# Layer-1 context attention of a four-layer perceiver: every product but the scores split into two column halves

## The chip, the cores and the metric

The kernel runs on one core of one Trainium2 chip. A core has a matrix engine (TensorE, which the profile splits into PE, the products, and PEld, the loads of the stationary operand), a vector engine (DVE), a scalar engine (ACT), a general engine (POOL) and a queue engine that issues transfers (SP). TensorE multiplies with an array of 128 rows and 128 columns and writes into PSUM, a memory of eight banks. The rows stand for the summed index and the columns for the output's partitions. A product that needs only a part of the array can be placed in that part; the profile writes "128*64" for a product that uses 128 rows and 64 columns.

The metric is device time in microseconds, the median of several runs.

## The reference, cut to what matters

The program is a perceiver with four layers. Each layer lets 2 x 256 queries of width 256 attend over a context, then over themselves, then runs a feed-forward block. Here only layer 1's attention over the context matters. It has 16 heads of width 64 and 4096 context rows per batch:

```python
def _L1_xattn_setup():
    B, S, D = (4, 512, 256)
    H, DK, DV = (16, 64, 64)
...
x = x + _L1_xattn_ref(_layernorm(x, axis=-1), ctx_1024, ctx_1024,
                      L1_xattn_Wq, L1_xattn_bq, L1_xattn_Wk, L1_xattn_bk,
                      L1_xattn_Wv, L1_xattn_bv, L1_xattn_Wo, L1_xattn_bo)
```

For each head: q = xn Wq + bq, k = ctx Wk + bk, v = ctx Wv + bv, softmax(q k^T) v, and the heads' outputs are multiplied by Wo and added up. Everything is in fp32.

## The kernel before, in words

The method `l1_xattn` (from L973 on) works on pairs of heads: a pair fills 128 partitions, one head in the lower 64 and one in the upper 64. There are n = 16 pairs (8 per batch; `u` counts them), and each pair's 4096 context rows are taken in 8 pieces of 512, so there are G = 128 pieces, counted by `g`. The nested functions are the stages of a piece:

- `keys(g)`: kT (128 x 512) from the transposed context, two products of 512 columns, then ACT adds the bias (L1024).
- `scores(g)` (L1051): both heads side by side in the row halves of the array, since a head has only 64 rows to sum over; four PSUM banks. ACT copies the scores out (L1058), DVE keeps a running maximum (L1061).
- `less(g)`: DVE adds the negative maximum (L1072), ACT takes the exponential (L1075), POOL adds up the sums (L1086; in the last pair DVE and L1082 share this).
- `values(g)`: v (4 x 128 rows by 128) from the context, eight products of 128 columns.
- `weigh(g)` (L1098): both heads side by side in the column halves of the array, since a head has only 64 output columns.
- Once per pair: `query` makes the queries; `combine`, `turned` (L1119, four transposes), `maxima` (L1125) and `repeat` (L1130, four transposes) turn the maximum of each query into a row that `less` can add; the sums of exponentials come from a product with ones; `end` divides (L1135, L1136, L1139), and `out` multiplies by Wo.

Products go through the helper `mm` (L358), so keys, values, query, out and sums all bear that line; the transposes of `turned` and `repeat` are calls of the transpose operation. Every fp32 product is two records in the profile, with a load each; a transpose is one.

The loop at L1158 writes the order out by hand, and `in_order` (L1157) fixes it for PE, DVE, ACT and POOL. In step g it issues `weigh(g-10)`, then `out` (when g % 8 is 2) or `query` (5), half of `less(g-9)`, `end` (1), `keys(g+1)`, `turned` (0), the other half of `less(g-9)`, `maxima` (0), `values(g-9)`, `repeat` (0) and `scores(g)`. The stage has PSUM banks 4 "mm" (scores, query, turned, sums, out), 2 "tr" (keys, values), 1 "acc" (weigh) and 1 "dec" (repeat). Context pieces are loaded by SP three steps ahead (L1006). In the first steps there is nothing to weigh; after step 128 there are only values, weigh and less.

Of the kernel before, what the change touches and what calls it, by code (L numbers as in the profile page):

```python
# [22 lines left out]
P = 128  # L23
B = 2
L = 256
# [4 lines left out]
KC = D // P  # L30
# [238 lines left out]
class Perceiver:  # L269
# [85 lines left out]
    def mm(self, out, pairs):  # L355

        for i, (lhsT, rhs) in enumerate(pairs):
            self.nc.tensor.matmul(out, lhsT, rhs, start=i == 0, stop=i == len(pairs) - 1)  # L358
# [614 lines left out]
    def l1_xattn(self, x, cpool):  # L973
# [9 lines left out]
        nc = self.nc  # L983
        with ExitStack() as s:
# [3 lines left out]
            xnT = self.to_T(self.layernorm(x))  # L988
            wq, wk, wv, wo = (self.weight(f"l1x_w{n}") for n in "qkvo")
# [8 lines left out]
            halves = [slice(0, 64), slice(64, 128)]  # L998
            order = [(hh, i) for i in range(2) for hh in range(2)]
            ctx, q, kT, v, score = {}, {}, {}, {}, {}  # L1000
            most, low, spread, total, av, sums, rec, z = {}, {}, {}, {}, {}, {}, {}, {}
# [7 lines left out]
            def for_values(g):  # L1009

                return ("k", g + 8) if g + 8 < G and (g + 8) // 64 == g // 64 else ("v", g)

            def query(u):
                ps = self.bank([P, L])
                self.mm(ps, [(wq[:, k, ts(u % 8, P)], xnT[:, k, ts(u // 8, L)]) for k in range(KC)])
                q[u] = p2.tile([P, L], F32, name="qT", tag="qT")
                return lambda: nc.vector.tensor_scalar_add(q[u], ps, self.col("l1x_bq", u % 8))

            def keys(g):
                pr = g // 8 % 8  # L1020
                ps = self.bank([P, 512], "tr")
                self.mm(ps, [(wk[:, k, ts(pr, P)], ctx["k", g][:, k, :]) for k in range(KC)])
                kT[g] = p2.tile([P, 512], F32, name="kT", tag="kT")
                nc.scalar.activation(kT[g], ps, AF.Identity, bias=self.col("l1x_bk", pr))  # L1024

            def values(g):
                pr = g // 8 % 8
                ps = self.bank([P, 4, P], "tr")
                for i in range(4):
                    self.mm(  # L1030
                        ps[:, i, :],
                        [(ctx[for_values(g)][:, k, ts(i, P)], wv[:, k, ts(pr, P)]) for k in range(KC)],
                    )
                v[g] = p2.tile([P, 4, P], F32, name="v", tag="v", bufs=3)
                self.copy(g < G - 8, v[g], ps)
# [80 lines left out]
            def turned(u):  # L1116
                ps = self.bank([P, 4, P])
                for i in range(4):
                    nc.tensor.transpose(ps[:, i, :], low[u][:, i // 2, ts(i % 2, P)], self.ident)  # L1119
                low[u] = ps  # L1120

            def maxima(u):
# [18 lines left out]
            def out(u):  # L1141
                ps = self.bank([P, 2, D])
                for qt in range(2):
                    self.mm(ps[:, qt, :], [(z[u][:, ts(qt, P)], wo[:, u % 8, :])])
                two = y[:, ts(u // 8, 2), :]
                return lambda: nc.vector.tensor_add(two, ps, two)

# [9 lines left out]
            with self.in_order(e.PE, e.DVE, e.Activation, e.Pool):  # L1157
                for g in range(-1, G + 12):  # L1158
# [7 lines left out]
                    u = g // 8 - 1 if g % 8 == 0 and 0 < g <= G else None  # L1166
# [6 lines left out]
                    if g % 8 == 2 and made(g - 11):  # L1173
                        evacs.append(out((g - 11) // 8))
                    if (g == -1 or g % 8 == 5) and made(g + 3):
                        evacs.append(query((g + 3) // 8))
# [5 lines left out]
                    if made(g + 1):  # L1182
                        keys(g + 1)
                    if u is not None:
                        turned(u)
# [6 lines left out]
                    if made(g - 9) and g <= G:  # L1192
                        values(g - 9)
                    if made(g - 8) and g >= G:
                        values(g - 8)
# [1394 lines left out]
```

## Time and profile before

| what | value |
|---|---|
| median of 3 runs | 2627.32 us (2615.05, 2627.32, 2627.75) |
| profiled execution's own time | 2616.86 us |
| its span, first to last instruction | 2615.1 us |
| mean granted TensorE clock | 0.96 (1.00 from 360 to 1236 us) |
| busy share of the span: PE, DVE, ACT, POOL | 95%, 66%, 51%, 35% |
| layer 1's context attention | about 263 to 1299 us of the span |
| its keys (PE, L358) | 512 records of 128x512, 250.6 us busy |
| its values (PE, L358) | 2048 records of 128x128, 249.9 us busy |
| its scores (PE, L1051) | 2048 records of 64x256, 255.7 us busy |
| its weigh (PE, L1098) | 2048 records of 128x256, 250.1 us busy |

Times in a profile are those of one execution. A group line names source line, engine, operation, output and inputs, shape and count. A timeline line begins with the start (us from the span's start) and the length of a run of equal instructions; the end of its last product is modelled, so the next group may start before it. In square brackets stands the idle time of the engine just before, and what ended it.

### The profile page before, as it was taken

To read this page: it belongs to the slowest core of one execution; us is meant where nothing else is said; L and a number is where in the kernel's file an instruction comes from. 1 tells how busy PE (TensorE), PEld (TensorE's weight loads), DVE (VectorE), ACT (ScalarE), POOL (GpSimd) and SP (SyncE) were. 2 spreads that over 40 slices of the span, in tenths; PEclk is the share of its full clock that TensorE was granted. 3 is DMA by queue.
4 is the path that set the end of the run, shared out by engine and by line. 5 is a ranking of instruction groups with operands and counts; after the bars stand their busy time and mean duration, and the time that the engine had idled before them with its cause. 6 is when DMAs were issued, how large, how long until landed. Compare 5 with 4: busy or idle time off the path is not lost.

```text
span 2615.1 us, 45590 instructions
## 1 busy us (share of the span) xinstructions
PE 2480.0 (95%) x17701; PEld 1659.1 (63%) x17701; DVE 1713.5 (66%) x3184; ACT 1343.4 (51%) x2540; POOL 919.3 (35%) x864
## 2 busy tenths in 40 slices
PE   8987999999999999999799998899989999999889
PEld 6854566666666666666533565556935666664678
DVE  5566577777777777777769755544267888854642
ACT  3323666666666666666466421432215777784512
POOL 0520255555555555556639413001101222210010
PEclk9988999999999999999899998789999999999889
DMA  6210322222232222222210100005730000003656
GB/s 256 89 57 30 118 65 65 67 72 65 65 113 82 70 69 65 65 67 81 80 65 1 65 20 22 4 25 214 266 147 18 2 2 2 2 2 123 218 213 223
DMA packets 77255, 214.24 MB, mean 82 GB/s; under 512 B 6408, under 2 KB 21456, under 8 KB 66544
## 3 DMA queue, kind: packets, MB, share of 16 engines
q1 hardware_dynamic: 72128, 202.69, 23.4%
q0 software_dynamic: 1888, 5.90, 0.7%
q8 instruction: 139, 2.28, 0.4%
q10 hardware_dynamic: 3024, 2.75, 0.3%
q14 instruction: 76, 0.62, 0.1%
HBM read 190.48 MB, written 20.84 MB: 81 GB/s over the span
## 4 chain that ended last, share of the span: by engine, by line
PE 39%; DVE 6%; issue 2%; ACT 2%; POOL 2%; DMA 0%; another core or an unknown queue 0%; DVEq 0%; ACTq 0%; POOLq 0%; SPq 0%
PE ps_mm L358 10%; PE ps_mm L2172 5%; PE ps_tr L2216 5%; PE ps_tr L2200 4%; PE ps_tr L358 3%; PE acc L358 3%; PE ps_mm L785 2%; DVE state L1357 1%; POOL spread L1345 1%; PE ps_tr L2335 1%; PE acc L826 1%; PE ps_tr L801 1%; PE ps_tr L2378 1%; PE ps_mm L2360 1%; PE acc L1583 1%
## 5 line engine op out<-in xcount | busy, mean ns | idle before, releaser
L1086 POOL TENSOR_TENSOR total<-total,S 128x512 f32<-128x512 f32 x434 | 540.8, 1278 | 299.6 <-ACT S L1075 299.2
L1075 ACT ACTIVATE S<-S 128x512 f32<-128x512 f32 x512 | 302.3, 625 | 209.0 <-DVE S L1072 208.8
L2176 DVE TENSOR_REDUCE mx<-ps_mm 128x1 f32<-128x512 f32 x512 | 317.9, 684 | 73.0 <-PE ps_tr L2200 54.2
L1061 DVE TENSOR_TENSOR most<-ps_mm,most 128x512 f32<-128x512 f32 x448 | 278.3, 684 | 119.2 <-ACT S L1058 119.2
L1058 ACT COPY S<-ps_mm 128x512 f32<-128x512 f32 x512 | 262.8, 600 | 115.3 <-PE ps_mm L1051 114.5
L1072 DVE TENSOR_TENSOR S<-S,ps_dec 128x512 f32<-128x512 f32 x512 | 317.6, 680 | 1.3 <-PE ps_dec L1130 1.3
L2204 ACT ACTIVATE PT<-ps_tr 128x512 f32<-128x512 f32 x476 | 246.7, 603 | 74.6 <-PE ps_tr L2200 71.8
L358 PEld LDWEIGHTS ps_tr<-w_l1x_wv,ctxT 128*128 128x128 f32 x2048 | 246.9, 192 | 52.5 <-issue 52.2
L1051 PE MATMUL ps_mm<-qT,kT 64*128 64x256 f32 x2048 | 255.7, 389 | 0.0
L1098 PE MATMUL acc<-S,v 128*64 128x256 f32 x2048 | 250.1, 385 | 0.5 <-DVE rec L1136 0.4
L358 PE MATMUL ps_tr<-ctxT,w_l1x_wk 128*128 128x512 f32 x512 | 250.6, 612 | 0.0
L2172 PE MATMUL ps_mm<-kT,qT 32*128 32x512 f32 x1024 | 250.1, 618 | 0.2 <-DVE mx L2176 0.2
L358 PE MATMUL ps_tr<-w_l1x_wv,ctxT 128*128 128x128 f32 x2048 | 249.9, 275 | 0.0
L2200 PE MATMUL ps_tr<-qm,kT 32*128 32x256 f32 x1904 | 238.3, 388 | 0.0
L1051 PEld LDWEIGHTS ps_mm<-qT,kT 64*128 64x128 f32 x2048 | 187.3, 186 | 38.3 <-DVE most L1061 3.8
L1098 PEld LDWEIGHTS acc<-S,v 128*64 128x64 f32 x2048 | 136.1, 136 | 97.3 <-ACT S L1058 38.8
L2200 PEld LDWEIGHTS ps_tr<-qm,kT 32*128 32x128 f32 x1904 | 171.0, 184 | 15.6 <-issue 6.2
L2225 POOL TENSOR_TENSOR sums<-sums,part 128x256 f32<-128x256 f32 x102 | 73.7, 722 | 257.1 <-ACT part L2224 257.1
L358 PEld LDWEIGHTS ps_tr<-ctxT,w_l1x_wk 128*128 128x128 f32 x512 | 89.2, 189 | 100.6 <-issue 99.1
L335 DVE COPY v<-ps_tr 128x512 f32<-128x512 f32 x120 | 82.9, 690 | 89.0 <-PE ps_tr L358 88.9
L2216 PE MATMUL ps_tr<-PT,v 128*32 128x256 f32 x2048 | 139.6, 385 | 0.3 <-ACT PT L2204 0.3
L2172 PEld LDWEIGHTS ps_mm<-kT,qT 32*128 32x128 f32 x1024 | 86.3, 185 | 61.3 <-issue 49.9
(542 smaller groups left out, 3808.8 us busy)
## 6 DMA issues: line engine op xcount, KB each, us to landing
ctxT<-in_ctxT SPq DMA_DIRECT2D x144, 512.0 KB, 3.6
ctxT<-in_ctxT SPq DMA_DIRECT2D x16, 1024.0 KB, 5.7
w_l2f_gu<-in_l2f_gu SPq DMA_DIRECT2D x16, 1024.0 KB, 7.1
bd_dram<-bd SPq DMA_DIRECT2D x8, 1536.0 KB, 5.5
w_l3f_w<-in_l3f_w SPq DMA_DIRECT2D x11, 1028.0 KB, 9.8
w_l3f_w<-in_l3f_w SPq DMA_DIRECT2D x11, 1024.0 KB, 5.1
ctx<-in_ctx SPq DMA_DIRECT2D x8, 1024.0 KB, 4.9
w_l2f_down<-in_l2f_down SPq DMA_DIRECT2D x16, 512.0 KB, 5.3
```

The source lines that it names most:

```text
L358: self.nc.tensor.matmul(out, lhsT, rhs, start=i == 0, stop=i == len(pairs) - 1)
L1051: nc.tensor.matmul(banks[hh, i][:, j, :], k[part, ts(2 * i + j, P)], q[u][part, :], start=True, stop=True)
L1058: nc.scalar.copy(t, ps)
L1061: nc.vector.tensor_tensor(m, ps, m, ALU.max)
L1072: nc.vector.tensor_tensor(t, t, spread[u][:, hh, :].unsqueeze(1).to_broadcast([P, 2, L]), ALU.add)
L1075: nc.scalar.activation(t, t, AF.Exp)
L1086: nc.gpsimd.tensor_add(tot, tot, t)
L1098: nc.tensor.matmul(av[u][part], vs[:, 2 * i + j, part], got[hh, i][:, j, :], start=g % 8 == 0 and i + j == 0, stop=g % 8 == 7 and i + j == 2,)
L2172: nc.tensor.matmul(ps, qT[rows, 2 * half + c, ts(t, P)], kT[rows, ts(j, 512)], start=True, stop=True,)
L2176: nc.vector.tensor_reduce(mx[:, c, r, j : j + 1], ps, AX.X, ALU.max)
L2200: nc.tensor.matmul(ps[:, i, :], kT[rows, ts(2 * u + i, P)], q[rows], start=True, stop=True)
L2216: nc.tensor.matmul(ps[ts(r, 32), :], v[:, 2 * u + i, :], pt[:, i, :], start=i == 0, stop=i == 1)
```

## The change

A local `mm` takes the place of the helper in `query`, `keys`, `values`, `turned` and `out`. It splits the stationary operand's 128 columns into two halves of 64 and the output's partitions likewise, and issues the two halves of each pair of operands one after the other; both halves stream the same second operand. `turned` no longer uses the transpose operation: it multiplies the maxima (stationary) by the identity. `scores`, `weigh`, the sums and `repeat` are as they were.

```diff
+            def mm(ps, pairs):
+
+                for k, (a, b) in enumerate(pairs):
+                    for part in halves:
+                        nc.tensor.matmul(ps[part], a[:, part], b, start=k == 0, stop=k == len(pairs) - 1)
+
             def query(u):
                 ps = self.bank([P, L])
-                self.mm(ps, [(wq[:, k, ts(u % 8, P)], xnT[:, k, ts(u // 8, L)]) for k in range(KC)])
+                mm(ps, [(wq[:, k, ts(u % 8, P)], xnT[:, k, ts(u // 8, L)]) for k in range(KC)])
...
             def keys(g):
                 pr = g // 8 % 8
                 ps = self.bank([P, 512], "tr")
-                self.mm(ps, [(wk[:, k, ts(pr, P)], ctx["k", g][:, k, :]) for k in range(KC)])
+                mm(ps, [(wk[:, k, ts(pr, P)], ctx["k", g][:, k, :]) for k in range(KC)])
...
                 for i in range(4):
-                    self.mm(
+                    mm(
                         ps[:, i, :],
                         [(ctx[for_values(g)][:, k, ts(i, P)], wv[:, k, ts(pr, P)]) for k in range(KC)],
                     )
...
             def turned(u):
                 ps = self.bank([P, 4, P])
                 for i in range(4):
-                    nc.tensor.transpose(ps[:, i, :], low[u][:, i // 2, ts(i % 2, P)], self.ident)
+                    mm(ps[:, i, :], [(low[u][:, i // 2, ts(i % 2, P)], self.ident)])
                 low[u] = ps
...
             def out(u):
                 ps = self.bank([P, 2, D])
                 for qt in range(2):
-                    self.mm(ps[:, qt, :], [(z[u][:, ts(qt, P)], wo[:, u % 8, :])])
+                    mm(ps[:, qt, :], [(z[u][:, ts(qt, P)], wo[:, u % 8, :])])
```

## The prediction

> **What bounds the kernel now.** I first looked up the stage that the change touches, the layer-1 context attention, which runs from 263 us (first L358 key product) to 1299 us of the span. The busy times by window give its steady part:
>
> ```profile
> 360.00:1236.00 876.00, 874.83 (x6043) 606.00 (x6042) 654.14 (x1047) 547.58 (x1003) 511.81 (x412) 1.00 0.25 72
> ```
>
> Columns: window, length, then PE, PEld, DVE, ACT, POOL busy (instructions), granted clock, DMA share, GB/s. TensorE is busy 874.8 of 876.0 us, VectorE, the next, 654 (75%). So time here is TensorE's time, and the question is what lies between its instructions, since a busy PE is not PE at its peak. The timeline of one ordinary step g, TensorE alone:
>
> ```profile
> 787.09 1.95 PE L1098 MATMUL acc<-S,v 128*64 128x256 f32 x16
> 788.96 1.98 PE L358 MATMUL ps_tr<-ctxT,w_l1x_wk 128*128 128x512 f32 x4
> 790.78 1.95 PE L358 MATMUL ps_tr<-w_l1x_wv,ctxT 128*128 128x128 f32 x16
> 792.66 2.00 PE L1051 MATMUL ps_mm<-qT,kT 64*128 64x256 f32 x16
> ```
>
> The next weigh starts at 794.59: a step lasts 7.50 us: weigh 1.87, keys 1.82, values 1.88, scores 1.93. The array's shape (rows*columns in use) is 128*64, 128*128, 128*128, 64*128: three changes of shape per step. Their price shows in two other places of the same view, where one of these groups has a neighbour of its own shape:
>
> ```profile
> 1254.63 1.95 PE L1098 MATMUL acc<-S,v 128*64 128x256 f32 x16
> 1256.41 1.08 PE L358 MATMUL ps_mm<-total,ones 128*64 128x256 f32 x8
> ...
> 822.03 1.88 PE L358 MATMUL ps_tr<-ctxT,w_l1x_wk 128*128 128x512 f32 x4
> 823.75 1.95 PE L358 MATMUL ps_tr<-w_l1x_wv,ctxT 128*128 128x128 f32 x16
> ```
>
> Weigh followed by the sums (128*64 too) takes 1.78, not 1.87; keys after the 128*128 product of `out` take 1.72, not 1.82. So the change of shape from weigh to keys costs 0.09 before the first key product and 0.10 after it, 0.20 us in the single records (0.310 instead of 0.213 to the first start, 0.533 instead of 0.429 to the second). The instructions by tile confirm the second half (min/median/max ns):
>
> ```profile
> L358 PEld LDWEIGHTS ps_tr<-w_l1x_wv,ctxT x2048: 186/192/192, 305.1 to 1284.5; 128*128 128x128 f32 x187
> L358 PE MATMUL ps_tr<-w_l1x_wv,ctxT x2048: 272/275/377, 305.5 to 1284.6; 128*128 128x128 f32 x187
> L358 PE MATMUL ps_tr<-ctxT,w_l1x_wk x512: 592/592/697, 262.7 to 1236.4; 128*128 128x512 f32 x171
> ```
>
> The longest key product, the one behind a change, is 105 ns over the median.
>
> **What the Trainium skill says.** "TensorEngine Tiling (Array Packing)", Tiling Modes: changing the tiling mode, not merely the tile, drains TensorE. The trace agrees (0.20 us above, none between weigh and sums). The same page, Restrictions: column tiling excludes the transpose mode for fp32; this is why the change turns `low` by products, and no run here shows it. "TensorE: Matmul & The Clock Gate", LDWEIGHTS: load time follows the columns, P/1.2 ns, so 107 ns for 128 and 53 for 64; the trace has 192 and 137 ns (L358, L1098), a difference of 55: it agrees. The same page, Part 1 ("Wait — 56ns, not 53.3ns?"): without hardware decode the sequencer spends about 62 ns per MATMUL; the trace has 32 MATMULs in 1.08 us (34 ns, L2390), so that bound does not hold here.
>
> **The change part by part.** DVE, ACT, POOL and SP issue the same instructions in the same order with the same waits. Only TensorE's stream differs: each 128-column product becomes two 64-column ones. A call is two records, loads beside it, so an ordinary step gets 20 more matmuls (4 keys, 16 values) and 20 more loads.
>
> *Streaming* is equal if halves overlap. Weigh already runs pairs, 7 ns apart, a pair every 216 ns at 256 columns, against 214 for one full product (`out`, `query`). At 512 columns the 128*32 products of L2134 come in every 429 ns, as full key products do. Keys: 0 saved. `out` and `query`: 4 x 1.3 ns lost, 28 times, 0.1 us.
>
> *Values* have 128 columns to stream and 128 to load, and start every 111.6 ns. The nearest row with less to load is L2390, four 32-column tiles of 128 streamed, every 109.1 ns. I take that for pairs: 16 x 2.5 = 0.04 us per step. Bounds: 0 if the load is not what holds them, 0.08 at 106.7.
>
> *Weigh to keys* (or to `out`, `query`, or sums to keys) no longer changes shape: 0.205 us per step. Values to scores and scores to weigh still do: 2 changes remain of 3.
>
> So an ordinary step falls from 7.50 to 7.26 us. They are g = 10..127 without the multiples of 8: 118 - 14 = 104, and 104 x 0.244 = 25.4 us.
>
> *Steps with g a multiple of 8* turn the maxima: four L1119 transposes (start to start 0.44 us in all) become 8 pairs of 109 = 0.87 us, +0.44; keys start 0.205 earlier, values save 0.04: TensorE ends values 0.19 later. Then `repeat`, still 128*128 transposes, adds a change of shape, 0.1 before its first product. What it waited for before:
>
> ```profile
> 807.52 0.68 DVE L1125 TENSOR_REDUCE nm<-ps_mm 128x4 f32<-128x512 f32 x1
> ...
> 808.26 0.41 PEld L1130 LDWEIGHTS ps_dec<-ident,nm 128*128 128x128 f32 x4 [0.27 <-DVE nm L1125]
> ```
>
> The reduce ends at 808.20, and its chain (most, low, less, nm) hangs on the scores before, not on this step's products; the maxima are turned about 1 us before it reads them. Values' last product was at 807.90, so `repeat` could have begun at 808.02; now 808.02 + 0.19 + 0.1 = 808.31, 0.05 late; with the rest of the change I take 0.07. 14 x 0.07 = 1.0 us lost. If that cover were gone it would be 0.3 each.
>
> *g = 8 and g = 128*: here TensorE waits for `low` itself (idle 1.23 and 1.73 us), so the 0.44 stands open: -0.45 and, with the new change of shape, -0.5.
>
> *Head, g = 0..7*: scores to keys changes shape before and after, but then loads 64 columns; the longest L1098 product is 52 ns over its median, not 105: 8 x 0.05 = +0.4.
>
> *Tail, g > 128*: nothing. The closing sums wait 3.62 us for POOL's last L1086 at 1292.3, and POOL's additions follow `repeat` of the last pair. Faster values there only wait longer.
>
> Sum: 25.4 + 0.4 - 0.1 - 1.0 - 1.0 = 23.7 us. The profiled execution took 2616.9 us (span 2615.1), so 2593.2 for its like. The median of the three runs, 2627.3, lies 10.4 above it, one run (2615.05) below; I subtract from the median: **2603.6 us**.
>
> New waits: keys now also wait for TensorE's own products of a step before, 32 products back, long done. Behind them stand values and scores, so it would matter if it were not.
>
> **The rivals.**
> *Nearly all arrives* (0.74): 20 to 27 us, 2600 to 2607; with runs like the fastest of before, from 2589.
> *Another engine or the issue eats half* (0.13). For: values become 64 loads and products in 1.75 us, 27 ns each, and if each takes over 31 ns, the 0.24 is gone. Against: L2390's stretch has 64 in 1.08 us; but the longest dense stretches average only 31 to 33 ns over 8 to 16 us, where other waits mix in. VectorE's slack is about 0.5 us per step (its last `less` ends some 6.8 us after a scores start, values 7.3), over the 0.24 needed; right after the reciprocal (1.75 us, L1135) it is close to nothing, once in 8 steps. Gain 8 to 16, 2611 to 2619.
> *The gap is not the shape* (0.08): it belongs to the wait in front of keys, and stays. Against: the sums also wait, for ACT and POOL, and start without a gap. Then only values' 5 us less 2: 2624.
> *Slower* (0.05): two halves that stream the same rows do not overlap. Every side-by-side group in this trace streams different data into its tiles, so this is not shown. Serial keys and values would add 1.72 + 1.75 = 3.5 us to each of 128 steps, 444 us, 3070; it decides from 7% of overlap lost (0.244 of 3.5). Against: 4 tiles with 4 streams run at full rate.
>
> **How the numbers follow.** About 0.5% (13 us) is what a measurement here can tell; the three runs lie 12.7 apart. Of the first case nearly nine in ten are clearly faster (0.9% mean), of the second half: faster 0.80, same 0.15 (the third case, half the second, some of the first), slower 0.05. Range 2588 to 2615: it leaves out part of the second case and the last two.
>
> **What would show it.** In the changed profile, in an ordinary step: weigh to keys 1.78, keys 1.72, values 1.84, the step 7.26; the weigh-to-keys idle of weight loads gone, that before scores and weigh still there; `repeat` no longer idle on `nm`, steps with turning as long as before or 0.1 longer; POOL's wait in front of the last sums unchanged. Wrong if value pairs are over 112 ns apart, if partners start over 20 ns apart, or if TensorE's idle on VectorE or ScalarE grows by more than 5 us in the stage.

## The result

| | before | changed |
|---|---|---|
| median, us | 2617.87 (2615.05 to 2627.75, 5 runs) | 2595.28 (2593.83 to 2599.01, 5 runs) |
| ratio | | 0.9904, 95% interval 0.9883 to 0.9924 |
| span of the profiled execution, us | 2615.1 | 2593.2 |
| start of the first `query` product to start of the last sums, us | 1032.53 | 1010.37 |
| ordinary step, us | 7.503 | 7.268 |
| step that turns the maxima, us | 8.676 | 8.723 |

The kernel is about 1% faster: the medians are 22.6 us apart (20 to 31 us by the interval of the ratio), and the predicted difference was 23.7. The whole time is too coarse to tell these apart, so the account below goes by the stage in the two profiles. The stage alone accounts for 22.2 us of the two profiles' 21.9; the rest of the program differs by 0.3 the other way. (The median of before fell from 2627.3 to 2617.9 when two runs were added; its runs scatter over 12.7 us, so an absolute prediction made from three of them was 8 us too high while the difference was right.)

Busy time by window, changed kernel, steady part of the stage (window, length, then PE, PEld, DVE, ACT, POOL busy, granted clock, DMA share, GB/s):

```profile
360.00:1215.00 855.00, 855.00 (x8513) 587.56 (x8513) 654.05 (x1048) 546.83 (x1005) 513.15 (x413) 1.00 0.25 74
```

TensorE has no idle time at all in this window; VectorE, the next, has the same 654 us of work in 855 instead of 876 us. So no other engine took over. The timeline of an ordinary step, TensorE alone:

```profile
781.89 1.95 PE L1104 MATMUL acc<-S,v 128*64 128x256 f32 x16
783.66 1.89 PE L1017 MATMUL ps_tr<-ctxT,w_l1x_wk 128*64 128x512 f32 x8
785.38 1.92 PE L1017 MATMUL ps_tr<-w_l1x_wv,ctxT 128*64 128x128 f32 x32
787.23 2.00 PE L1057 MATMUL ps_mm<-qT,kT 64*128 64x256 f32 x16
```

From start to start: weigh 1.77 (before 1.87), keys 1.72 (1.82), values 1.85 (1.88), scores 1.92 (1.93). Twice as many key and value records take no more time, so the halves overlap in full although both stream the same data: in the single records (the start times of the products one by one) partners start 7 ns apart, key pairs every 429 ns and value pairs every 109 ns. The instructions by tile (min/median/max ns):

```profile
L1017 PEld LDWEIGHTS ps_tr<-w_l1x_wv,ctxT x4096: 132/137/137, 304.8 to 1259.0; 128*64 128x64 f32 x196
L1017 PE MATMUL ps_tr<-w_l1x_wv,ctxT x4096: 272/273/317, 305.2 to 1259.1; 128*64 128x128 f32 x196
...
L1017 PE MATMUL ps_tr<-ctxT,w_l1x_wk x1024: 592/592/644, 262.3 to 1212.5; 128*64 128x512 f32 x171
```

A load for values takes 137 ns instead of 192, and the longest key product is 52 ns over the median instead of 105. The weight loads show the changes of shape that are left:

```profile
787.23 1.60 PEld L1057 LDWEIGHTS ps_mm<-qT,kT 64*128 64x128 f32 x16 [0.17 <-issue]
789.15 1.49 PEld L1104 LDWEIGHTS acc<-S,v 128*64 128x64 f32 x16 [0.33 <-ACT S L1064]
790.72 0.36 PEld L1017 LDWEIGHTS ps_tr<-ctxT,w_l1x_wk 128*64 128x64 f32 x4
```

Into scores and into weigh the loads are idle as before. Into keys, where they were idle 0.39 us, no idle time is printed any more; the first is issued while weigh still runs.

### The profile page after: what moved, and what is told of

It reads as the page before. It is cut to its first block, busy times and chain, and to the rows that moved or that the text cites. A ratio compares the mean times of both kernels' runs of the same rounds, so it can differ in the third digit from the quotient of the medians.

```text
span 2593.2 us, 51423 instructions
## 1 busy us (share of the span) xinstructions
PE 2456.4 (95%) x20579; PEld 1640.5 (63%) x20581; DVE 1711.2 (66%) x3184; ACT 1342.3 (52%) x2540; POOL 921.6 (36%) x864
## 4 chain that ended last, share of the span: by engine, by line
PE 40%; DVE 6%; ACT 2%; issue 2%; POOL 2%; DMA 0%; DVEq 0%; ACTq 0%; POOLq 0%; SPq 0%
PE ps_mm L358 10%; PE ps_mm L2178 5%; PE ps_tr L2222 5%; PE ps_tr L2206 4%; PE ps_tr L358 3%; PE acc L358 3%; PE ps_mm L785 2%; DVE state L1363 1%; POOL spread L1351 1%; PE ps_tr L2341 1%; PE acc L826 1%; PE ps_tr L2384 1%; PE ps_tr L801 1%; PE acc L1589 1%; PE ps_tr L434 0%
## 5 line engine op out<-in xcount | busy, mean ns | idle before, releaser
L1017 PEld LDWEIGHTS ps_tr<-w_l1x_wv,ctxT 128*64 128x64 f32 x4096 | 235.4, 137 | 58.3 <-issue 57.7
L1017 PE MATMUL ps_tr<-w_l1x_wv,ctxT 128*64 128x128 f32 x4096 | 248.2, 273 | 0.0
L1017 PE MATMUL ps_tr<-ctxT,w_l1x_wk 128*64 128x512 f32 x1024 | 242.4, 593 | 0.0
L1017 PEld LDWEIGHTS ps_tr<-ctxT,w_l1x_wk 128*64 128x64 f32 x1024 | 75.8, 137 | 91.0 <-issue 75.3
```

The costliest lines, as they stand in the source:

```text
L1017: nc.tensor.matmul(ps[part], a[:, part], b, start=k == 0, stop=k == len(pairs) - 1)
```

## The experiments

**e1: keys, `query` and `out` in halves, values and `turned` as before.** It takes away the change of shape between weigh and keys and puts one between keys and values, so it tells the shape from the place.

```diff
             def values(g):
...
-                    mm(
+                    self.mm(
...
             def turned(u):
...
-                    mm(ps[:, i, :], [(low[u][:, i // 2, ts(i % 2, P)], self.ident)])
+                    nc.tensor.transpose(ps[:, i, :], low[u][:, i // 2, ts(i % 2, P)], self.ident)
```

(against the changed kernel)

> Keys, query and out in column halves; values whole and turned by transposes, as before. My theory (a change of the array's shape costs, wherever it stands): weigh to keys falls from 1.87 to 1.78 us and the first key product is no longer late, but keys to values becomes a change of shape, so values get 0.2 us longer in their lead-in; three changes per step as before, the ordinary step stays 7.50 (7.48 to 7.52), the whole within 5 us of the kernel before. Rival (the gap belongs to the wait in front of keys, or to the heavier load of keys alone): lighter keys alone bring 0.2 us per step, step 7.30, 20 us or more in all.

Measured: 2617.76 us against 2622.39 for the kernel before on the same chip, ratio 0.9987 (0.9977 to 0.9998). The ordinary step takes 7.503 us, to the nanosecond what it took before. Its timeline on TensorE:

```profile
787.45 1.89 PE L1017 MATMUL ps_tr<-ctxT,w_l1x_wk 128*64 128x512 f32 x8
789.27 2.05 PE L358 MATMUL ps_tr<-w_l1x_wv,ctxT 128*128 128x128 f32 x16
791.25 2.00 PE L1057 MATMUL ps_mm<-qT,kT 64*128 64x256 f32 x16
793.18 1.95 PE L1104 MATMUL acc<-S,v 128*64 128x256 f32 x16
794.95 1.46 PE L1017 MATMUL ps_tr<-ctxT,w_l1x_wk 128*64 128x512 f32 x6
```

Weigh to keys is 1.77, as in the changed kernel; but keys take 1.82 again and values 1.98, 0.10 more than before. The 0.2 us moved from one border to the next. What costs is the change of shape, wherever it stands; neither the wait in front of keys nor the lighter load of keys brings anything alone. (The medians are 4.6 us apart, 0.5 to 6 us by the interval of the ratio. This does not lie in the stage of the profiled executions, which lasts 1032.34 us from first `query` to last sums, against 1032.53; its cause is not known.)

**e2: values alone in halves.** It adds a change of shape instead of removing one. Of the change it keeps only the local `mm` and its use in `values`; `query`, `keys`, `out` and `turned` are those of before:

```diff
+            def mm(ps, pairs):
+
+                for k, (a, b) in enumerate(pairs):
+                    for part in halves:
+                        nc.tensor.matmul(ps[part], a[:, part], b, start=k == 0, stop=k == len(pairs) - 1)
...
                 for i in range(4):
-                    self.mm(
+                    mm(
                         ps[:, i, :],
...
```

(against the kernel before)

> Only values in column halves; keys, query, out and turned as before. Shape theory: now four changes per step (weigh to keys, keys to values, values to scores, scores to weigh). The added one enters a 64-column shape, 0.15 us; values give back 16 x 2.5 ns = 0.04. Ordinary step 7.61 us, 104 of them +11 us, steps with turning +0.1 each: 10 to 14 us slower than before, ratio about 1.005. Rival (the gain of the change comes from the lighter loads of values, not from the shape): 4 to 5 us faster than before, step 7.46.

Measured: 2636.56 us, ratio 1.0047 (1.0028 to 1.0066), 12 us slower by the ratio and 14 by the medians. The ordinary step takes 7.617 us, expected 7.61, and steps 10 to 127 together 11.4 us more than before. (In its profiled execution, the longest of the five, the stage is 18.5 us longer; the rest lies outside these steps, where the trace shows half the clock from 304.6 to 308.0 and from 1267.2 to 1270.6 us, spells that the profile of before does not have.) Steps with turning stayed at 8.677 where +0.1 was expected, since `repeat` waits for VectorE there. So lighter loads for values, bought with a fourth change of shape, lose. Over e2, e1 and the changed kernel the sign follows the number of changes of shape: 4 slower, 3 the same, 2 faster.

**e3: the changed kernel with `turned` by transposes again.** It tells what the longer products of `turned` cost.

```diff
-                    mm(ps[:, i, :], [(low[u][:, i // 2, ts(i % 2, P)], self.ident)])
+                    nc.tensor.transpose(ps[:, i, :], low[u][:, i // 2, ts(i % 2, P)], self.ident)
```

> The changed kernel with turned by four transposes again, so 0.44 us less products in 16 steps but two more changes of shape there (keys to turned 0.2, turned to values 0.15). Theory: the step with turning falls from 8.72 to 8.68, because repeat then waits for the reduce on VectorE again; at g = 8 about 0.4 us is regained, at g = 128 about 0.2; 1 us faster than the changed kernel in all, not to be told from it by its time. If turned were the main loss of the change, 16 x 0.44 = 7 us faster.

Measured: 2596.48 us, ratio to before 0.9899 (0.9882 to 0.9915); by time it cannot be told from the changed kernel (0.9904, 0.9883 to 0.9924). The step with turning takes 8.676 us, expected 8.68, and the stage is 1.5 us shorter in its profile than the changed one's (1008.83 against 1010.37): 0.65 in the steps with turning, 0.55 ahead of the first weigh, where g = 8 lies, and 0.30 at g = 128. The weight loads in front of `repeat`, changed kernel:

```profile
792.39 1.06 PEld L1017 LDWEIGHTS ps_mm<-ident,low 128*64 128x64 f32 x16 [0.45 <-issue]
793.41 1.78 PEld L1017 LDWEIGHTS ps_tr<-w_l1x_wv,ctxT 128*64 128x64 f32 x32
795.37 0.41 PEld L1136 LDWEIGHTS ps_dec<-ident,nm 128*128 128x128 f32 x4 [0.17 <-DVE nm L1131]
```

and in e3:

```profile
792.02 0.42 PEld L1125 LDWEIGHTS ps_mm<-ident,low 128*128 128x128 f32 x4 [0.81 <-issue]
...
794.60 0.41 PEld L1136 LDWEIGHTS ps_dec<-ident,nm 128*128 128x128 f32 x4 [0.26 <-DVE nm L1131]
```

In e3 the load comes 0.02 us behind the reduce's end: VectorE sets it. In the changed kernel the reduce ends at 795.26 (L1131, 794.58 + 0.68) and the load follows 0.11 later, 0.2 behind the last value product, the length of a change of shape: here TensorE sets it, by some 0.05 us. The profile still prints DVE as the one that ended the wait. The products for `turned` cost 0.44 us more and the two changes of shape in e3 about 0.3 (0.29 in the single records), and VectorE's chain hides either but for these 0.05 us.

**e5: the changed kernel with the two loops of `mm` exchanged.** It asks how much of the result hangs on the partners being neighbours.

```diff
-                for k, (a, b) in enumerate(pairs):
-                    for part in halves:
+                for part in halves:
+                    for k, (a, b) in enumerate(pairs):
```

> The changed kernel with the two loops of its mm exchanged: of each call all products of the lower half are issued, then all of the upper half, so partners stand two calls (four records) apart in the order instead of one (two records). If TensorE finds the other half's product behind them, as the sums seem to show (their halves are issued like this and their records still come in pairs), nothing changes: step 7.27 us, ratio 0.990. If partners must be neighbours, keys and values run one half after the other in part: each call of two products loses a half's last products, keys +0.4 to 1.7 us, values +0.2 to 1.7 us a step, 80 to 440 us slower than the changed kernel.

Measured: 2603.34 us, ratio to before 0.9915 (0.9897 to 0.9933). The ordinary step takes 7.320 us, 0.052 more than in the changed kernel. The halves still overlap in full, as e5's timeline on TensorE shows for a group's values (start, length, then the group of records):

```profile
792.43 1.97 PE L1017 MATMUL ps_tr<-w_l1x_wv,ctxT 128*64 128x128 f32 x32
```

These 32 records take 1.90 us to the next start, against 1.85. But from the second pair of key products on, partners start 50 to 59 ns apart instead of 7, and the step waits once for the half that is behind. Most of the time is kept; "nothing changes" was a little too bold.

**e6: the values' halves far apart**, all eight calls of the lower half before those of the upper.

```diff
-                for i in range(4):
-                    mm(
-                        ps[:, i, :],
-                        [(ctx[for_values(g)][:, k, ts(i, P)], wv[:, k, ts(pr, P)]) for k in range(KC)],
-                    )
+                for part in halves:
+                    for i in range(4):
+                        for k in range(KC):
+                            nc.tensor.matmul(
+                                ps[part, i, :], ctx[for_values(g)][:, k, ts(i, P)][:, part], wv[:, k, ts(pr, P)],
+                                start=k == 0, stop=k == KC - 1,
+                            )
```

> The changed kernel with the values alone issued in another order: all eight calls of the lower half (16 records), then all eight of the upper half, so partners stand 16 records and as many loads apart; keys, query, out and turned keep neighbours. Exchanging the loops within one call (partners four records apart) had cost 0.05 us a step. If TensorE keeps work for each half and runs past the waiting one over that distance, values take 1.85 to 2.0 us and the step stays under 7.4. If it sees fewer than 32 records and loads ahead, the lower half begins alone and the upper ends alone: for a reach of r of the 16 records the values take (2 - r/16) x 1.75 us, at r = 8 2.6 us, at r = 0 3.5; step 8.1 to 9.0, 90 to 200 us slower than the changed kernel.

Measured: 2757.96 us, ratio to before 1.0523 (1.0487 to 1.0559). The ordinary step takes 8.628 us, 1.36 more than in the changed kernel, all of it in values:

```profile
832.58 1.89 PE L1017 MATMUL ps_tr<-ctxT,w_l1x_wk 128*64 128x512 f32 x8
834.29 3.28 PE L1038 MATMUL ps_tr<-w_l1x_wv,ctxT 128*64 128x128 f32 x32
837.50 2.00 PE L1059 MATMUL ps_mm<-qT,kT 64*128 64x256 f32 x16
```

Values take 3.21 us. In the single records the first 12 starts lie 109 ns apart, alone; then come four pairs, 6 to 58 ns apart; and then the other 12, again 109 ns apart, alone. With the relation in the expectation, (2 - r/16) x 1.74 = 3.11 (the change of shape taken off), the reach r is 3 to 4 records with their loads. This also gives a floor for the price of the rival "the halves do not overlap": with most of the overlap gone, values alone cost 1.36 us a step.

## Why the prediction was right

The mechanism stands, and nearly each term came out at its size. From single records, in us (plus is a gain; the two rows on single steps are parts of the row below them and not added again):

| term | predicted | measured |
|---|---|---|
| stage start to first weigh (head and g = 8) | -0.1 | +0.1 |
| ordinary step, its length | 7.50 to 7.26 | 7.503 to 7.268 |
| step with turning, longer by | 0.07 | 0.046 |
| g = 10 to the weigh of g = 128 | +24.3 | +23.8 |
| g = 128, weigh to `repeat` | -0.5 | -0.71 |
| tail, `repeat` to the last sums | 0 | -1.0 |
| sum | 23.7 | 22.2 |

- *The price of a change of shape, 0.205 us from weigh to keys*: right, and shown by e1 and e2, not only argued. The parts (0.09 ahead of the first product, 0.10 after it, half of that when 64-column weights follow) are those that e2's 0.15 was made of.
- *Value pairs every 109 ns*, taken from L2390: measured 109. The bounds, 107 and 111.6, were not needed. Together with the first term this gave 0.244 per step; measured 0.235, the 0.01 in weigh and values.
- *Steps with turning are hidden by VectorE*: right in size and reason (0.05 late), shown by e3.
- *g = 8*: `turned` stood open there and its longer products were paid; the head's 0.05 per step made up for it, as predicted.
- *g = 128*: 0.21 more than predicted. The wait for `low` became longer. Changed kernel, TensorE's timeline (before: idle 1.73 at the same place):

```profile
1226.17 1.09 PE L1017 MATMUL ps_mm<-ident,low 128*64 128x128 f32 x16 [1.96 <-DVE low L1120]
```

  In the step before, VectorE's and ScalarE's work on the scores had not become shorter with TensorE's; the scores came 0.24 us sooner and had to wait: ScalarE, busy with the exponentials, begins to copy them 1.72 us after their first product (before: 1.49), without idle time in front. Where VectorE sets the pace, TensorE's gain is not kept.
- *Tail*: that POOL's additions set the end is right, and from `repeat` to the first closing sums it takes 38.44 us, before 38.29. But the step "faster values there only wait longer" was taken to cost nothing. Changed kernel:

```profile
1269.13 1.98 PE L358 MATMUL ps_mm<-total,ones 128*64 128x256 f32 x8 [5.89 <-POOL total L1092]
```

  TensorE had waited 3.62 us before and now waits 5.89, and the eight sums take 1.77 us to the next start instead of 0.93: their pairs start 426 to 479 ns apart where it was 215 to 267. The granted clock (the third number from the right) shows what changed. In the kernel before, at the eight sums and after them:

```profile
1292.39:1293.30 0.91, 0.91 (x8) 0.64 (x9) 0.00 (x0) 0.00 (x0) 0.00 (x0) 1.00 0.00 0
1293.38:1297.00 3.62, 1.78 (x6) 0.56 (x3) 1.77 (x2) 0.00 (x0) 0.00 (x0) 0.50 0.00 0
```

  In the changed kernel, early in the wait, and from then until the sums are done:

```profile
1263.00:1265.50 2.50, 0.24 (x2) 0.00 (x0) 0.00 (x0) 0.00 (x0) 2.42 (x3) 1.00 0.00 0
1265.60:1272.30 6.70, 3.17 (x12) 1.71 (x12) 0.00 (x0) 0.00 (x0) 3.48 (x3) 0.50 0.00 0
```

  Both waits were followed by half the clock, but before it came 4.6 us after TensorE had fallen idle, when the eight sums were through, and now it comes 2.3 us after, ahead of them (in e2, e3 and e5 3.5 to 4.1 us after, ahead of them too). The experiments have other waits at this place: after 1.68 us (e6) and 3.63 us (e1) the eight sums take 0.93 and 0.94 us, after 5.57 to 5.88 us (e2, e3, e5) 1.77 us each. The Trainium skill, "TensorE: Matmul & The Clock Gate", Part 1, has the clock fall to half after an idle window of about 3.4 us. The trace agrees on the half, and on a wait of 1.68 us leaving the clock whole; but in the changed kernel 2.3 us without work were enough. This is the term of the sum that was missing: 0.84 us.

The rivals: no other engine took over (TensorE busy 855.0 of 855.0 us); the issue of instructions did not bind at 27 ns each; the gap was the shape's (e1); the halves overlap while streaming the same rows (partners 7 ns apart), so the slower case did not come, but e6 shows that another order of the same products brings much of it back for values. None of the signs of being wrong showed in an ordinary step (value pairs 109 ns apart, partners 7), and TensorE's idle time on VectorE and ScalarE in the stage went from 6.0 to 5.4 us. Two of the other signs did not come as written: POOL's wait in front of the last sums grew instead of staying, and `repeat` still lists idle time on `nm`.

## What to carry to other kernels

When TensorE is the bound, list the array shapes of its products in the order of issue and count the changes: each cost about 0.15 us here where weights of 64 columns follow, and about 0.2 us where 128 columns follow. Bring neighbours to one shape even where a product would fit the whole array (splitting keys and values cost no time of its own here), and count the changes over the whole loop, since curing one border only (e1, e2) moves or adds a change. Issue the halves alternately: partners four records apart lost a little, sixteen apart for values made the whole kernel 5% slower than before.

## What the runs showed that I had not expected

The two column halves each run their own row of work, to a small distance. In the last steps of the changed kernel, where values and weigh follow each other without a change of shape, products of the two groups start in between each other (TensorE's timeline):

```profile
1239.87 1.79 PE L1017 MATMUL ps_tr<-w_l1x_wv,ctxT 128*64 128x128 f32 x27
1241.44 0.38 PE L1104 MATMUL acc<-S,v 128*64 128x256 f32 x1
1241.49 0.38 PE L1017 MATMUL ps_tr<-w_l1x_wv,ctxT 128*64 128x128 f32 x2
1241.66 0.38 PE L1104 MATMUL acc<-S,v 128*64 128x256 f32 x1
1241.71 0.27 PE L1017 MATMUL ps_tr<-w_l1x_wv,ctxT 128*64 128x128 f32 x1
```

The loop issues all 32 value products before the next weigh, yet the first weigh starts ahead of three of them. The records do not name the half. But those of one half lie 109 ns apart in values and 216 in weigh, so one half is already at weigh, from 1241.44 on, while the other finishes its values and comes to weigh at 1241.82, 0.38 us behind. So products of different column halves do not always start in the order of issue. The Trainium skill, "TensorE: Matmul & The Clock Gate", The mechanism, has them start and end strictly in program order; the starts in this trace differ from that. So do those of e5 and e6, where products 50 to 59 ns apart must belong to two halves although several of one half are issued in a row. The distance over which one half can overtake the other is short, 3 to 4 records in e6.
